# Token loads, low parts and the start of a conditioned transformer block: four edits of order

## The chip, the cores and the metric

The kernel runs on one core of one Trainium2 chip. Its time is the device time of one execution in microseconds (us); where several runs were made, their median is given. The engines are TensorE (PE; PEld is its weight load), VectorE (DVE), ScalarE (ACT), GpSimd (POOL) and SyncE (SP). SP here does nothing but issue DMA transfers; ACT and POOL issue some too. Each engine works through its own instructions in order.

## The reference

One block of a diffusion transformer on x of 2 x 2048 x 512 with a condition of 2 x 512, all in f32:

```
mod = silu(condition) @ Wada + bada            # 512 -> 6 * 512
sh_a, sc_a, gt_a, sh_m, sc_m, gt_m = split(mod, 6)
xm = layernorm(x, g1, be1) * (1 + sc_a) + sh_a
x  = x + gt_a * attention(xm)                  # 16 heads of 32, causal
xm = layernorm(x, g2, be2) * (1 + sc_m) + sh_m
x  = x + gt_m * (gelu(xm @ W1 + b1) @ W2 + b2) # 512 -> 2048 -> 512
```

attention(xm) is xm @ Wqkv (512 -> 1536) split into q, k and v, softmax(q k^T / sqrt(32)) v with the causal mask, and a projection with Wproj and bproj.

## The kernel before

**Stages.** The two batch rows run one after the other. For each: queries, keys and values are made (`Qkv.run`, L1138) while the first scores already run; then the attention phase; the projection of row 0 is done in row 1's start (L1531). At the end comes the MLP for both rows.

**Products.** A 512-wide product is split into halves and made by seven half products in place of eight (the four blocks of a matrix are A11, A12, A21, A22, and S1 to S4 are sums of them, L886). Weight sums are made on GpSimd, sums of tokens on VectorE. One unit of such a product is seven steps (`unit`, L1002) into three banks ps_a, ps_b and ps_c. Banks are emptied by ScalarE (first, direct) and VectorE (last).

**Qkv.run.** Four groups g of 512 tokens; in each, four units of keys and queries and two of values, 42 steps. After each step comes `tick` (L1145), which places other work by hand: at n = 3 the loads of the next group's tokens (`load_x`, L915, four tiles "x" from four buffers, on SP), at n = 10 to 13 their statistics on VectorE, at n = 15 and 25 their scaling on ScalarE (x, L964), at 18 and 28 the transposes on TensorE (ps_xt) with the modulation into xmT (L274), at 36 to 40 sums of tokens; also scores (`row.score`), and one load of stored keys or queries for the scores. `load_x` is called for g + 1 at n = 3 if it hasn't been yet. A group whose statistics, tiles or weights are late holds what stands behind it in its queue.

**hi and lo.** Keys and queries are stored as a rounded high part and a low part (`split`, L1061): hi is a cast on ScalarE (L1064), lo = value - hi is made at L1066, on VectorE for groups 0 and 1 and on GpSimd for groups 2 and 3. There are three hi buffers, so a fourth hi waits until the first is stored and its lo made. SP stores both to DRAM (L1031).

**Pieces.** MLP weights are summed ahead of time inside `Qkv.run` (class Pieces): `load` (L1222 to L1243) puts the loads of four blocks on SP, `add` puts sums on GpSimd (L1251) and stores to w1d or w2d (L1271). In `tick` (L1275) one or two of these operations are issued. A plan gives each piece the tick of its load and of its first sum. In row 1 the last piece (room_3) is loaded at tick 74 and summed from tick 80 on.

**Order.** Instructions passed through `mm`, `act` or `transpose` (L204 to L214) keep the order in which they are written on their engine; the others are placed by a scheduler. DMA transfers issued by SP and ACT share eight completion counters, one after the other in turn.

**The start** (L1360 to L1490). ScalarE issues loads of the condition and of g1, be1, g2, be2, b1, b2 into one tile `rows`, with `first`, a one-column Sqrt, at L136. SP loads the tokens of group 0, eight tiles of Wada (named vv, since they lie in room of vv), Wqkv's four blocks (wqk, L926) and the values' four (wv, L936). `rows` is transposed (ps_c, L1401) and copied to `cols`. ScalarE makes Silu of the condition from `cols` into sc (L1455); TensorE multiplies it with Wada (ps_mod, `modulation`, L1406), VectorE adds the bias (mr, L1425), TensorE turns the result into columns (ps_modt), and `scale_shift` (L1440) makes a and c, by which the transposed tokens become xmT (L269, L274). Then come the first products (ps_qk). GpSimd sums the weights column block by column block (L944).

The functions that the diff touches:

Of the kernel before, what the change touches and what calls it, by code (L numbers as in the profile page):

```python
# [8 lines left out]
F32 = mybir.dt.float32  # L9
# [8 lines left out]
P = 128  # L18
# [9 lines left out]
def dit_block_kernel(  # L28
# [104 lines left out]


    first = const.tile([P, 1], F32, tag="first", name="first")
    nc.scalar.activation(first, eps, AF.Sqrt)  # L136


    cols = const.tile([P, 64], F32, tag="cols", name="cols")
# [68 lines left out]
    def act(ins):  # L208

        return tc.keep_in_program_order(ins)  # L210
# [687 lines left out]
    class Qkv:  # L898
# [21 lines left out]
                xts.append(xt)  # L920
            self.xts[g] = xts

        def load_w(self, queue):
            for n, i, k in BASE:
                act(
                    queue.dma_start(  # L926
                        self.w[:, n], w_v[:, k * HK : (k + 1) * HK, i * D : (i + 1) * D]
                    )
                )

# [110 lines left out]
        def keys_and_queries(self, g, f, hp):  # L1041

            ops = self.operands(g)
            los = [self.lo_tile(hp) for _ in range(2)]

            def part(i, j):
                return los[i].bitcast(F32)[:, j * HALF_T : (j + 1) * HALF_T]

            def product(ps, n, new):
                for k in range(HK):  # L1050
                    mm(
                        ps, self.w[:, n, k, f * P : (f + 1) * P], ops[n][:, k],
                        start=new and k == 0, stop=k == HK - 1,
                        skip_group_check=not new,
                    )

            def first(ps, i, j):
                scale = HD**-0.5 if i == 0 else 1.0
                nc.scalar.activation(part(i, j), ps, AF.Copy, scale=scale)

            def split(i):  # L1061
                hi, lo = self.hi_tile(hp), los[i]
                d = lo.bitcast(F32)
                nc.scalar.copy(hi, d)  # L1064
                engine = nc.vector if g < 2 else nc.gpsimd
                engine.tensor_tensor(lo, d, hi.bitcast(F32), ALU.subtract)  # L1066
                self.stored(g, f, i, (hi, lo))

            def last(ps, i, j):
                d = part(i, j)  # L1070
                if i == 0:
                    nc.vector.scalar_tensor_tensor(
                        d, ps, HD**-0.5, d, ALU.mult, ALU.add
                    )
                    if j == 0:
                        split(0)
                else:
                    nc.vector.tensor_tensor(d, d, ps, ALU.add)

            def direct(ps, i, j):  # L1080
                first(ps, i, j)
                split(1)

            return self.unit(product, first, last, direct)
# [53 lines left out]
        def run(self, hp, also, early=()):  # L1138
# [3 lines left out]
            for g in range(NG):  # L1142
                at = [0]

                def tick():  # L1145
                    n, at[0] = at[0], at[0] + 1
                    if n >= self.STEPS:
                        return
                    if g + 1 < NG:
                        if n == 3 and g + 1 not in self.xts:  # L1150
                            self.load_x(g + 1)
                        if 10 <= n < 10 + MTT and g + 1 > row.b:
                            self.stats(g + 1, n - 10)
                        if n in (15, 25):
                            self.scaled(g + 1, n // 25)
                        if n in (18, 28):
                            self.norm(g + 1, n // 28)()
                        sums = {36: S1, 38: S2, 40: S3}
                        if n in sums:
                            self.token_sum(g + 1, sums[n])  # L1160
                    elif n == 28:

                        row.rows(0)
                        act(nc.scalar.activation(first, eps, AF.Exp))
                    if g > 0 and n == 2:
                        self.token_sum(g, A22)
                    if n > 9 and self.loads:
                        self.loads.pop(0)()
                    also(g, n)
                    if g > 0 and n >= 7:  # L1170


                        past, of = n - 6, self.STEPS - 7
                        if g == 1:
                            row.score(row.count(cum[0] * past / of, 0))
                        else:
                            past += of * (g - 2)
                            row.score(
                                row.count(
                                    cum[0] + (cum[2] - cum[0]) * past / (2 * of),  # L1180
                                    1 if g == 2 and n < 25 else 2,
                                )
                            )

                for u in range(C + 2):
                    if (g, u) in early:
                        for k, step in enumerate(self.plain(g, u, hp)):
                            step()
                            if k:
                                tick()  # L1190
                        self.token_sum(g, S3)
                        continue
                    if u < C:
                        steps = self.keys_and_queries(g, u, hp)
                    else:
                        steps = self.values(g, u - C)
                    for step in steps[:2] + late + steps[2:6]:
                        step()
                        tick()
                    late = steps[6:]  # L1200
# [159 lines left out]
    with pool("wada") as wp, pool("qkv0") as qp, pool("hl0") as hp, pool(  # L1360
        "ps_qkv0", bufs=6, space=PSUM
    ) as ps_mm:
        rows = wp.tile([n_rows, P], F32, tag="rows", name="rows")
        for r, n, src in (
            (0, n_cond, cond.rearrange("b (c p) -> (b c) p", p=P)),
            (r_g1, C, g1.rearrange("(c p) -> c p", p=P)),
# [3 lines left out]
            (r_b1, FC, b1.rearrange("(c p) -> c p", p=P)),  # L1370
            (r_b2, C, b2.rearrange("(c p) -> c p", p=P)),
        ):
            nc.scalar.dma_start(rows[r : r + n, :], src)
        wada_v = Wada.rearrange("(c p) f -> p c f", p=P)
        wada = {}

# [17 lines left out]
        qkv = Qkv(row, qp, ps_mm)  # L1394
        qkv.load_x(0)
        load_wada(0, 1)
        qkv.load_w(nc.sync)
        qkv.load_wv(hp, nc.sync)

        ps_c = ps_mm.tile([P, n_rows], F32, tag="mm", name="ps_c")  # L1400
        transpose(ps_c, rows)  # L1401
        nc.vector.tensor_copy(cols[:, :n_rows], ps_c)
        sc = wp.tile([P, C, HD], F32, tag="sc", name="sc")
        nc.vector.memset(sc, 0.0)

# [34 lines left out]
        def scale_shift(a, c, r_g, r_be, shift, scale):  # L1440
# [6 lines left out]
                )  # L1447
            nc.vector.tensor_tensor(c, c, mod[:, shift], ALU.add)

        for t in range(MTT):  # L1450
            qkv.stats(0, t)
        halves = [qkv.norm(0, 0, True)]

        act(
            nc.scalar.activation(  # L1455
                sc[:, :, :B], col(0, n_cond).rearrange("p (b c) -> p c b", c=C), AF.Silu
            )
        )
        picks()
        columns = modulation(0)  # L1460
        halves.append(qkv.norm(0, 1, True))
        columns()
        scale_shift(a1, c1, r_g1, r_be1, 0, 1)
        for k in range(0, C, 2):
# [862 lines left out]
```

## Time and profile before

| | |
|---|---|
| median of 3 runs | 2258.35 us (2256.87 to 2260.15) |
| profiled execution, own time | 2256.73 us |
| its span in the trace | 2255.0 us, 1.7 us lie outside the span |
| mean granted TensorE clock | 0.997 |
| TensorE busy | 2211.3 us, 98% |
| VectorE, ScalarE, GpSimd busy | 68%, 45%, 58% |

The page lists busy time and share of the span for each engine. In the chain of work that ended last, each instruction is followed back to what released it. In a timeline, rows have the start in us, the duration, the engine, the line, the operation with its tiles and sizes, the count of instructions grouped, and in brackets the idle time before with what ended it. A duration of a group runs from its first start to its last end. In the table by windows, each engine's column is its busy time with the number of instructions, then come the clock that TensorE was granted (1.00 is full), the share of DMA and the GB/s.

### The profile page before, as it was taken

The page shows a single profiled execution, that of the slowest core. Times are in us where ns is not written, and L with a number is a line of the kernel's source. Part 1 is how long each engine was busy: PE and PEld are TensorE (multiplying, and loading weights), DVE is VectorE, ACT ScalarE, POOL GpSimd, SP SyncE. Part 2 cuts the span into 40 slices and gives each one's busy share as a digit, 9 for nine tenths or more (in the row PEclk, how much of TensorE's full clock was granted, in tenths as well). Part 3 has the DMA queues.
Part 4 walks back from the last instruction along what each step waited for, and adds up shares of the span by engine and source line. Part 5 has one row for each costly group of instructions (what it writes and reads, how often), then busy time and mean ns, then how long its engine had stood idle before and what let it go on. Part 6 is the DMA issues. An engine that isn't in the chain of part 4 may idle for free.

```text
span 2255.0 us, 33464 instructions
## 1 busy us (share of the span) xinstructions
PE 2211.3 (98%) x12057; PEld 1432.2 (64%) x12057; DVE 1535.7 (68%) x3309; ACT 1004.6 (45%) x2012; POOL 1297.9 (58%) x807
## 2 busy tenths in 40 slices
PE   7999999999999999999999999999999999999998
PEld 6777555555543587855555555345787787688687
DVE  4668766777757666777577767663685586576576
ACT  4434555555564244365656555614322422332410
POOL 4253998998983695199989898444205204304210
PEclk9999999999999999999999999999999999999999
DMA  8877143231324799542324113363353354353433
GB/s 281 251 259 193 43 93 75 62 85 48 106 97 135 252 308 313 142 92 62 85 67 104 44 48 131 109 231 129 109 175 133 123 184 145 108 187 126 158 125 110
DMA packets 160510, 311.57 MB, mean 138 GB/s; under 512 B 16544, under 2 KB 48844, under 8 KB 158552
## 3 DMA queue, kind: packets, MB, share of 16 engines
q1 hardware_dynamic: 155488, 285.53, 41.8%
q0 software_dynamic: 4480, 23.36, 2.7%
q8 instruction: 95, 1.56, 0.3%
q14 instruction: 71, 0.58, 0.1%
q10 hardware_dynamic: 376, 0.55, 0.1%
HBM read 229.95 MB, written 87.29 MB: 141 GB/s over the span
## 4 chain that ended last, share of the span: by engine, by line
PE 89%; DVE 4%; DMA 2%; POOL 2%; ACT 1%; issue 1%; SPq 0%; DVEq 0%; ACTq 0%; POOLq 0%
PE ps_a L206 27%; PE st L206 18%; PE ps_b L206 12%; PE o L206 10%; PE s L206 9%; PE ps_c L206 4%; PE ps_o L206 4%; PE sm L206 3%; DVE junk L498 1%; POOL ee L695 1%; PE ps_xt L214 1%; DMA x<-in_x_dram 1%; ACT e L670 1%; DVE mx L504 1%; PE ps_o L214 1%
## 5 line engine op out<-in xcount | busy, mean ns | idle before, releaser
L670 ACT ACTIVATE e<-st 128x512 f32<-128x512 f32 (+1 forms) x1152 | 575.0, 579 | 362.4 <-PE st L206 321.3
L504 DVE TENSOR_REDUCE mx<-s 128x1 f32<-128x512 f32 x576 | 381.9, 686 | 199.0 <-PE s L206 197.9
L695 POOL TENSOR_TENSOR ee<-ee,e 128x2048 f32<-128x2048 f32 x106 | 485.8, 4583 | 10.3 <-ACT e L670 4.3
L206 PE MATMUL st<-qst,kst 128*128 128x512 f32 (+3 forms) x1280 | 408.7, 386 | 0.0
L206 PE MATMUL s<-kst,qst 128*128 128x512 f32 (+3 forms) x1046 | 382.2, 396 | 8.0 <-DVE mx L498 2.7
L206 PE MATMUL ps_a<-sum,w 128*128 128x256 f32 (+1 forms) x1088 | 328.8, 431 | 0.1
L206 PE MATMUL o<-e,vv 128*32 128x512 f32 (+3 forms) x2560 | 293.2, 537 | 0.3 <-POOL e L682 0.3
L206 PEld LDWEIGHTS st<-qst,kst 128*128 128x128 f32 x1280 | 228.5, 188 | 97.3 <-issue 65.7
L498 DVE CUSTOM_DVE_ANT_0 junk<-s,causal 128x128 bf16<-128x128 f32 (+3 forms) x470 | 220.7, 470 | 61.0 <-PE s L206 46.8
L1795 POOL TENSOR_TENSOR sum<-w 128x256 f32<-128x256 f32 x30 | 21.8, 727 | 397.1 <-DMA w<-w1d 203.1
L206 PEld LDWEIGHTS s<-kst,qst 128*128 128x128 f32 x1046 | 195.4, 189 | 72.4 <-DVE mx L504 15.4
L206 PEld LDWEIGHTS ps_a<-sum,w 128*128 128x128 f32 x1088 | 204.5, 190 | 40.1 <-issue 11.4
L695 POOL TENSOR_TENSOR ee<-e 128x2048 f32<-128x2048 f32 x42 | 192.5, 4583 | 43.5 <-ACT e L670 42.5
L206 PEld LDWEIGHTS <-sel 32*128 32x128 bf16 x1152 | 29.5, 91 | 197.0 <-issue 196.1
L2014 ACT ACTIVATE h<-h,cols 128x512 f32<-128x512 f32 x120 | 76.8, 710 | 136.3 <-DVE h L1716 136.3
L504 DVE TENSOR_REDUCE mx<-st 128x1 f32<-128x512 f32 x192 | 131.0, 682 | 0.5
L682 POOL TENSOR_SCALAR_AFFINE_SELECT e<-e 128x512 f32<-128x512 f32 x128 | 83.3, 669 | 67.2 <-ACT e L670 67.2
L206 PE MATMUL st<-fold,sel 32*128 32x512 bf16 (+1 forms) x1152 | 117.3, 372 | 1.2
L206 PEld LDWEIGHTS o<-e,vv 128*32 128x32 f32 x2560 | 59.1, 108 | 92.3 <-issue 72.8
L1716 DVE TENSOR_TENSOR h<-c,ps_b 128x256 f32<-128x256 f32 x90 | 37.9, 421 | 103.5 <-PE ps_b L206 103.0
L1066 POOL TENSOR_TENSOR lo<-lo,hi 128x512 fp32r<-128x512 f32 x32 | 40.7, 1274 | 114.2 <-ACT hi L1064 109.8
L206 PE MATMUL ps_b<-sum,w 128*128 128x256 f32 (+1 forms) x384 | 95.0, 383 | 0.0
(237 smaller groups left out, 3590.7 us busy)
## 6 DMA issues: line engine op xcount, KB each, us to landing
qst<-q SPq DMA_DIRECT2D x128, 256.0 KB
kst<-k SPq DMA_DIRECT2D x128, 256.0 KB
w<-w1d SPq DMA_DIRECT2D x32, 896.0 KB
w<-w2d SPq DMA_DIRECT2D x28, 1024.0 KB
w<-w2d SPq DMA_DIRECT2D x28, 768.0 KB
q<-hi SPq DMA_DIRECT2D x32, 256.0 KB
q<-lo SPq DMA_DIRECT2D x32, 256.0 KB
k<-hi SPq DMA_DIRECT2D x32, 256.0 KB
```

What stands on the lines that cost most here:

```text
L206: return tc.keep_in_program_order(nc.tensor.matmul(*args, **kw))
L214: return tc.keep_in_program_order(nc.tensor.transpose(dst, src, ident[:n, :n]))
L498: nc.vector.tensor_tensor_reduce(junk[:, :w], x, causal[:, QB - w :], 1.0, MASKED, ALU.add, ALU.max, m,)
L504: self.vector(nc.vector.tensor_reduce(m, x, axis=AX.X, op=ALU.max))
L670: act(nc.scalar.activation(e4[:, h, :w], sts[h][:, :w], AF.Exp))
L682: nc.gpsimd.affine_select(d, d, pattern=[[0, HC], [1, P]], compare_op=ALU.is_ge, fill=0.0, base=0, channel_multiplier=-1,)
L695: act(nc.gpsimd.tensor_tensor(dst, x, y, ALU.add))
L1066: engine.tensor_tensor(lo, d, hi.bitcast(F32), ALU.subtract)
L1716: act(nc.vector.tensor_tensor(dst, x, y, ALU.add))
L1795: act(engine.tensor_tensor(dst, u, v, op))
L2014: nc.scalar.activation(d[j], d[j], AF.Gelu, bias=col(r_b1 + half * HF + fs[j], 1))
```

## The change

Four edits of order, none of what is computed:

- **Tokens.** At n = 30 of group g, `tick` also loads the tokens of group g + 2, behind the last transposes (n = 28) of the tiles whose buffers they take. At n = 3 of the next group the load is then left out. The tokens of group 1 are loaded as before.
- **Low parts.** For groups 2 and 3 the subtraction on GpSimd is passed through `act` and so keeps its written place among GpSimd's other pinned work.
- **Start: condition.** A tile `rows_c` of its own takes the condition first (the load into `rows` stays), and ScalarE's loads are pinned, with a Silu of one column behind that of be1. `rows_c` is transposed into ps_1; Silu of it, straight from PSUM, and a Sqrt of one column behind it stand ahead of the statistics. The transpose of `rows` moves behind the second half of the first tokens. 36 transposes of the identity (`busy`) into ps_w go to TensorE before and behind ps_1.
- **Start: weights.** Wqkv's blocks are loaded by columns, 0 to 127, 128 to 255 and 256 to 511, in twelve transfers where there were four.

```diff
@@ -133,7 +133,6 @@
 
 
     first = const.tile([P, 1], F32, tag="first", name="first")
-    nc.scalar.activation(first, eps, AF.Sqrt)
 
 
     cols = const.tile([P, 64], F32, tag="cols", name="cols")
@@ -920,11 +919,12 @@
                 xts.append(xt)
             self.xts[g] = xts
 
-        def load_w(self, queue):
+        def load_w(self, queue, f=slice(0, D)):
             for n, i, k in BASE:
                 act(
                     queue.dma_start(
-                        self.w[:, n], w_v[:, k * HK : (k + 1) * HK, i * D : (i + 1) * D]
+                        self.w[:, n, :, f],
+                        w_v[:, k * HK : (k + 1) * HK, i * D + f.start : i * D + f.stop],
                     )
                 )
 
@@ -1063,7 +1063,9 @@
                 d = lo.bitcast(F32)
                 nc.scalar.copy(hi, d)
                 engine = nc.vector if g < 2 else nc.gpsimd
-                engine.tensor_tensor(lo, d, hi.bitcast(F32), ALU.subtract)
+                ins = engine.tensor_tensor(lo, d, hi.bitcast(F32), ALU.subtract)
+                if g >= 2:
+                    act(ins)
                 self.stored(g, f, i, (hi, lo))
 
             def last(ps, i, j):
@@ -1146,6 +1148,8 @@
                     n, at[0] = at[0], at[0] + 1
                     if n >= self.STEPS:
                         return
+                    if n == 30 and g + 2 < NG:
+                        self.load_x(g + 2)
                     if g + 1 < NG:
                         if n == 3 and g + 1 not in self.xts:
                             self.load_x(g + 1)
@@ -1361,6 +1365,7 @@
         "ps_qkv0", bufs=6, space=PSUM
     ) as ps_mm:
         rows = wp.tile([n_rows, P], F32, tag="rows", name="rows")
+        rows_c = wp.tile([n_cond, P], F32, tag="rowsc", name="rowsc")
         for r, n, src in (
             (0, n_cond, cond.rearrange("b (c p) -> (b c) p", p=P)),
             (r_g1, C, g1.rearrange("(c p) -> c p", p=P)),
@@ -1370,7 +1375,11 @@
             (r_b1, FC, b1.rearrange("(c p) -> c p", p=P)),
             (r_b2, C, b2.rearrange("(c p) -> c p", p=P)),
         ):
-            nc.scalar.dma_start(rows[r : r + n, :], src)
+            if not r:
+                act(nc.scalar.dma_start(rows_c, src))
+            act(nc.scalar.dma_start(rows[r : r + n, :], src))
+            if r == r_be1:
+                act(nc.scalar.activation(first, eps, AF.Silu))
         wada_v = Wada.rearrange("(c p) f -> p c f", p=P)
         wada = {}
 
@@ -1394,12 +1403,19 @@
         qkv = Qkv(row, qp, ps_mm)
         qkv.load_x(0)
         load_wada(0, 1)
-        qkv.load_w(nc.sync)
+        for f0, f1 in ((0, 1), (1, 2), (2, C)):
+            qkv.load_w(nc.sync, slice(f0 * P, f1 * P))
         qkv.load_wv(hp, nc.sync)
 
-        ps_c = ps_mm.tile([P, n_rows], F32, tag="mm", name="ps_c")
-        transpose(ps_c, rows)
-        nc.vector.tensor_copy(cols[:, :n_rows], ps_c)
+        ps_w = ps_sp.tile([P, P], F32, tag="s", name="ps_w")
+
+        def busy(n):
+            for _ in range(n):
+                transpose(ps_w, ident)
+
+        busy(6)
+        ps_1 = ps_sp.tile([P, n_cond], F32, tag="s", name="ps_1")
+        transpose(ps_1, rows_c)
         sc = wp.tile([P, C, HD], F32, tag="sc", name="sc")
         nc.vector.memset(sc, 0.0)
 
@@ -1447,18 +1463,23 @@
                 )
             nc.vector.tensor_tensor(c, c, mod[:, shift], ALU.add)
 
+        act(
+            nc.scalar.activation(
+                sc[:, :, :B], ps_1.rearrange("p (b c) -> p c b", c=C), AF.Silu
+            )
+        )
+        act(nc.scalar.activation(first, eps, AF.Sqrt))
+        busy(30)
         for t in range(MTT):
             qkv.stats(0, t)
         halves = [qkv.norm(0, 0, True)]
 
-        act(
-            nc.scalar.activation(
-                sc[:, :, :B], col(0, n_cond).rearrange("p (b c) -> p c b", c=C), AF.Silu
-            )
-        )
         picks()
         columns = modulation(0)
         halves.append(qkv.norm(0, 1, True))
+        ps_c = ps_mm.tile([P, n_rows], F32, tag="mm", name="ps_c")
+        transpose(ps_c, rows)
+        nc.vector.tensor_copy(cols[:, :n_rows], ps_c)
         columns()
         scale_shift(a1, c1, r_g1, r_be1, 0, 1)
         for k in range(0, C, 2):
```

## The prediction

> **What bounds the kernel now.** I read the busy shares first, then the chain of work that ended last, then TensorE's waits.
>
> ```profile
> PE 2211.3 (98%) x12057; PEld 1432.2 (64%) x12057; DVE 1535.7 (68%) x3309; ACT 1004.6 (45%) x2012; POOL 1297.9 (58%) x807
> PE 89%; DVE 4%; DMA 2%; POOL 2%; ACT 1%; issue 1%; SPq 0%; DVEq 0%; ACTq 0%; POOLq 0%
> ```
>
> TensorE is busy 98% of the span and carries 89% of the chain. No other engine is near it, and the change removes no product. So it can only move the little idle time that TensorE has, and the stretches at half clock behind such idle time. Both are in three places: the start, 118 us (row 0) and 873 us (row 1).
>
> ```profile
> PE ps_c L214 <- DMA rows<-in_L_cond_b_dram: 7.4, 1, 7.4
> PE ps_xt L214 <- ACT x L964: 5.6, 4, 3.8
> ```
>
> These are rows of the waits of 0 to 40 us and of 700 to 1000 us: total, times, longest. The first is not the start's real bound, since ps_c only feeds columns; the timeline is. Here are TensorE, ScalarE and SyncE's DMA issues at the start (start, us, engine and line, instructions, idle time before):
>
> ```profile
> 9.19 0.48 PE L214 MATMUL ps_xt<-ident,x 128*128 128x128 f32 x1 [1.50 <-ACT x L964]
> 11.58 2.75 PE L206 MATMUL ps_mod<-vv,sc 128*32 128x512 f32 x16
> 14.26 1.09 PE L214 MATMUL ps_xt<-ident,x 128*128 128x128 f32 x8
> 18.12 7.13 PE L206 MATMUL ps_qk<-xmT,wqk 128*128 128x512 f32 x16 [1.78 <-DVE xmT L269]
> 27.86 1.10 PE L206 MATMUL ps_a<-t,wqk 128*128 128x256 f32 x4 [0.89 <-POOL wqk L944]
> ...
> 2.40 0.32 ACTq L1373 DMA_DIRECT2D rows<-in_L_cond_be_dram  x1
> 4.32 1.28 ACT L136 ACT_TABLE_LOAD   x1 [4.32 <-DMA x<-in_x_dram]
> 5.61 0.20 ACT L136 ACTIVATE first<-eps 128x1 f32<-128x1 f32 x1
> 7.42 0.30 ACT L224 ACTIVATE rstd<-mv,eps 128x4 f32<-128x4 f32 x1 [1.61 <-DVE mv L221]
> 8.32 1.52 ACT L964 ACTIVATE x<-x,shift,rstd 128x512 f32<-128x512 f32 x2 [0.60 <-DVE shift L226]
> 11.15 0.21 ACT L1455 ACTIVATE sc<-cols 128x8 f32<-128x8 f32 x1
> ...
> 4.22 3.79 SPq L1391 DMA_DIRECT2D vv<-in_L_cond_Wada_dram  x8
> 12.18 0.37 SPq L936 DMA_DIRECT2D wv<-in_L_cond_Wqkv_dram  x1
> ```
>
> The reader is to see a chain on ScalarE: table load, rstd, scaled tokens, then the first transpose at 9.19, and 8.93 us later the first product of keys and queries (18.12).
>
> **The change, part by part. The start.** The hardware DMAs share eight completion counters in turn, and an issue waits until the load before it on its counter has landed. The trace shows it: ScalarE's table load at 4.32 stands behind a row load of b1 that waited for a token load, and the third value-weight load (12.18) was issued when the seventh Wada load had landed. The changed kernel pins the row loads and the first two activations to written order. As built, ScalarE's queue holds: condition twice, g1, be1, a Silu of one column, then g2, be2, b1, b2, then the Silu of the condition, Sqrt, rstd and the scaled tokens. The extra load turns the counters by one place, so that g2, be2, b1 and b2 now stand on those of the first, third, fifth and seventh Wada loads, and all of ScalarE's work stands behind the wait of b2. The seventh Wada load landed at 12.18. Before it DMA had a gap, in half-microsecond windows (busy time of each engine left to right, clock, DMA share, GB/s):
>
> ```profile
> 5.00:5.50 0.50, 0.00 (x0) 0.00 (x0) 0.27 (x2) 0.50 (x1) 0.41 (x1) 1.00 0.69 162
> 5.50:6.00 0.50, 0.00 (x0) 0.00 (x0) 0.32 (x1) 0.30 (x2) 0.00 (x0) 1.00 0.74 99
> 6.00:6.50 0.50, 0.00 (x0) 0.00 (x0) 0.47 (x2) 0.00 (x0) 0.00 (x0) 1.00 0.56 175
> 7.00:7.50 0.50, 0.11 (x1) 0.14 (x1) 0.47 (x4) 0.08 (x1) 0.00 (x0) 1.00 1.05 393
> ```
>
> Against 390 GB/s the three lack 228, 291 and 215 GB/s for 0.5 us each, 367 KB or 0.94 us. Without the counters' early waits SyncE issues sooner and the gap closes: landing at 12.18 - 0.94 = 11.2 (bounds 10.8, if the first issue at 4.22 moves up by its 1.35 us of waits, and 12.2, if nothing moves). Then: issue of b2 0.32, Silu 0.21, table load 1.28, first 0.20, rstd at 13.25; from rstd to the first transpose 9.19 - 7.42 = 1.77, so 15.0; then 8.93 to the first product, with one transpose (ps_c, 1.09 / 8 = 0.14) moved into it: 24.1, against 18.12, **+6.0**. The stall of 0.89 at 27.86, on GpSimd's weight sums, goes: the weights now come by columns and the products start 6 us later. That leaves **+5.1**. Bounds: +7.0 (landing at 12.2 and the stall kept); +2.5 (landing at 10.8, and the clock full from the first transpose on: eight transposes in 1.09 instead of the 2.4 from 9.19 to 11.58, ps_mod in 1.92 instead of 2.75).
>
> The 37 transposes of an identity run on TensorE while it would idle, done by 13 us at the latest (eight fill 9.19 to 11.58, 0.30 us each, so 37 take at most 11 us from about 2). They cost nothing, and I give them no gain: 2 us of idle time or more follow before 15.0, and at 118 us 2.75 us of idle time were enough for half clock (below). ScalarE's table load there stays one of 1.28.
>
> The Trainium skill's page "ScalarE: Activation LUTs", section "What ACT_TABLE_LOAD costs", puts a switch of table at 1.28 us of load and about 1.38 of drain; in this trace the row of 4.32 has the load, and the next activation starts 0.01 us behind it. By the page the start would be 1.4 us later than my sum.
>
> The page "TensorE: Matmul & The Clock Gate", section "Part 4: PE-mode transpose", says that transposes don't count as busy for the clock. By it ps_mod would run wholly at half clock. The trace speaks against it: at half clock its 16 matmuls would take twice the 1.92 us of 113.90 (below), 3.84, and they took 2.75, so the clock rose in the midst of them.
>
> **Row 0, near 118 us.** SyncE, VectorE, TensorE and the clock:
>
> ```profile
> 107.57 4.91 SPq L1230 DMA_DIRECT2D kst<-in_L_cond_W_dram  x4
> 112.58 1.84 SPq L919 DMA_DIRECT2D x<-in_x_dram  x4
> ...
> 118.51 0.69 DVE L218 BATCH_NORM_STATS2 stat<-x 128x6 f32<-128x512 f32 x1 [0.90 <-DMA x<-in_x_dram]
> ...
> 113.90 1.92 PE L206 MATMUL ps_mod<-vv,sc 128*32 128x512 f32 x16
> 119.86 0.80 PE L206 MATMUL s<-kst,qst 128*128 128x512 f32 x1 [2.75 <-DVE mx L498]
> ...
> 119.00:120.00 1.00, 0.14 (x1) 0.14 (x1) 1.00 (x5) 0.00 (x0) 0.00 (x0) 0.56 1.06 322
> 120.00:125.00 5.00, 5.00 (x12) 4.01 (x13) 3.58 (x10) 0.82 (x2) 1.45 (x2) 0.50 0.56 198
> 125.00:126.00 1.00, 1.00 (x4) 0.76 (x4) 0.72 (x3) 0.00 (x0) 0.92 (x2) 0.53 0.36 131
> ```
>
> The tokens of group 3 are issued behind four weight pieces; VectorE's statistics wait for them, and the maxima behind them hold TensorE 2.75 us. By the clock's column (third from the right) half clock lasts from 119.1 to 125.9, 6.8 us; from TensorE's start on that is (125.9 - 119.86) / 2 = 3.0 us lost. In the changed kernel the token load (tick 30) stands ahead of the four pieces, 5.0 us sooner. The third token tile, late at 118.51, is there at 113.5, before VectorE needs it. Its statistics also move earlier among the maxima, but wait for nothing. 2.75 + 3.0 = **-5.7** (-4.5 to -6.5: part of the stall kept, or the maxima before it sooner too). The pieces come 1.9 us later; GpSimd sums them behind other work.
>
> **Row 1, near 873 us.** SyncE, TensorE, GpSimd, ScalarE, clock:
>
> ```profile
> 861.25 0.93 SPq L1239 DMA_DIRECT2D vv<-in_L_cond_W_dram  x2
> 865.36 1.84 SPq L919 DMA_DIRECT2D x<-in_x_dram  x4
> ...
> 876.68 0.33 PE L214 MATMUL ps_xt<-ident,x 128*128 128x128 f32 x1 [3.79 <-ACT x L964]
> 884.26 1.89 PE L206 MATMUL ps_a<-t,wqk 128*128 128x256 f32 x8
> ...
> 867.51 1.27 POOL L1066 TENSOR_TENSOR lo<-lo,hi 128x512 fp32r<-128x512 f32 x1 [2.06 <-ACT hi L1064]
> 869.33 1.28 POOL L1251 TENSOR_TENSOR vv<-vv,kst 128x512 f32<-128x512 f32 x1 [0.55 <-DMA kst<-in_L_cond_W_dram]
> 881.55 0.56 POOL L1271 DMA_DIRECT2D w2d<-vv  x1
> 882.82 1.28 POOL L1251 TENSOR_TENSOR qst<-qst 128x128 f32<-128x128 f32 x3
> 887.73 3.73 POOL L1066 TENSOR_TENSOR lo<-lo,hi 128x512 fp32r<-128x512 f32 x3
> ...
> 881.39 0.62 ACT L1064 CAST hi<-lo 128x512 fp32r<-128x512 f32 x1 [0.44 <-POOL kst L1251]
> ...
> 877.00:880.00 3.00, 2.62 (x11) 2.43 (x11) 0.40 (x1) 2.71 (x6) 2.92 (x3) 0.50 0.94 188
> ```
>
> The same move brings the tokens 4.1 us forward (865.36 to 861.25), ahead of eight W2 pieces. The statistics no longer wait, but still stand in VectorE's order, one eviction of the product sooner; I take half of the wait of 3.79 as gone (1.9; bounds nothing and all of it), with the first transpose at 874.8. The half clock of 877 to 880 and about 0.4 us around it goes (3.4 / 2 = 1.7, estimated to go since 1.9 us of idle time are under the 2.75 at 118 us): TensorE would be **3.6 us** ahead near 881.
>
> The other edit takes it back. Each low part (lo) waits for its high part (hi, ScalarE); there are three tiles for hi, so a new hi waits until GpSimd has made an earlier lo. Before, the scheduler had put three lo ahead of the last W2 piece's sums (867.51 is the third). With the lo pinned to written order, the program has eleven sums ahead of the first lo, and four more ahead of the second. GpSimd now waits for W2 data which come 1.9 us later: sums from about 871.2 instead of 869.33, eleven in 881.55 - 869.33 = 12.2 us, so the first lo at 883.4 to 884.7, then one sum of kst and three of qst (in before from the end of the store at 882.1 to 884.1, 2.0 us) and the second lo (1.27): 888.0 at the latest, 886.7 at the earliest; I take 887.8. ScalarE's fourth and fifth hi wait for those, and in its queue stand ahead of two evictions (lo, 0.38 each) that TensorE needs for its ps_a: hi 0.62, evictions 0.7, so TensorE goes on at 889.1. In before it was at the same product at 885.1 (half of the row at 884.26): **+4.0**. It then has idled 7.5 us, and half clock follows, for 3.4 us (row 1 before) to 6.0 (row 0): half of it, +1.7 to +3.0; I take **+2.2**, nearer row 1's. Together **+6.2** for row 1. Bounds: -3.6 if nothing is held, +8.5 if the next hi, behind seven stores, holds TensorE again.
>
> **Sum.** +5.1 - 5.7 + 6.2 = +5.6 us on the profiled execution's 2256.73 (span 2255.0), so 2262.3; the median of the runs shown is 2258.35, 1.62 above it: **2264.0**. A measurement of this kernel tells about 0.2%, 4.5 us, from no change.
>
> **The rivals.**
>
> A second stall, chance 0.13. Behind the second lo stand one sum of 0.47 and seven stores (3.8 us) before the third (893.4), and hi 6 waits for it: TensorE loses 2 to 5 us more, or the start's later bound holds: 2268.
>
> The low parts hold nothing (the other side: not slower), 0.14. The evictions that TensorE needs pass before the waiting hi, so that GpSimd's new order costs only GpSimd. For it: GpSimd is busy 58%, and in before a hi at 881.39 already waited for GpSimd with TensorE unharmed. Against it: the queues run in order, and the lag of 12 us is longer than any slack here. It decides from the point where the first two lo end before 883. Row 1 is then -3.6: 2258.35 + 5.1 - 5.7 - 3.6 = 2254.2.
>
> ScalarE isn't held at the start, 0.07: the row loads pass without waiting for Wada. The first product then comes about 2 us sooner instead: 2258.35 - 2 - 5.7 + 6.2 = 2256.9. For it: Wada may land sooner than its issues tell. With the rival before, 2247: 0.04.
>
> The clock rises late at the start: no transpose counts for it, and ps_mod's 16 matmuls take 2 x 1.92 = 3.84 instead of 2.75, +1.1: 2265.1, chance 0.05. This is the rule of the Trainium skill's page on TensorE named above.
>
> The token load lands no sooner, since its buffers are still read at tick 30 and SyncE waits there: 0.03, 2264.0 + 5.7 = 2269.7.
>
> **How the numbers follow.** My forecast (2259 to 2268) has 0.54, of it 0.33 above 2262.9, with the late clock's 0.05, the second stall's 0.13 and the unmoved load's 0.03: slower 0.54. Faster, below 2253.8: 0.04 and half of the 0.14, 0.11. The rest, 0.35, is within 0.2%. The range, 2254 to 2270, leaves out the 0.04, some 0.07 of the rival around 2254.2, and the ends of the second stall.
>
> **What would show it.** Right: ScalarE's Silu of the condition at about 11.5 us, the first transpose of tokens near 15, the first ps_qk near 24; no wait of TensorE for VectorE's mx near 118, and clock 1.00 there; near 880 TensorE waiting 6 to 8 us for a lo on ScalarE, itself behind hi and GpSimd's W2 sums, and clock 0.50 after it. Wrong: a first ps_qk before 18; GpSimd's lo running between the sums; TensorE without a wait between 875 and 890; a new wait on the W2 pieces or on weights at 25 to 30 us.

## The result and the profile after

The changed kernel takes 2272.09 us (median of 5 runs, 2271.35 to 2273.83); the kernel before took 2258.85 in runs beside it (5 runs). The ratio is 1.0066 with a 95% interval of 1.0055 to 1.0077: some 15 us slower. The forecast was 2264.0, with a range up to 2270. The profiled execution took 2272.53 us, with a span of 2270.8 us; the mean granted clock fell from 0.997 to 0.993.

The page of the changed kernel, busy times and the chain that ended last:

```profile
PE 2220.8 (98%) x12094; PEld 1438.6 (63%) x12094; DVE 1530.7 (67%) x3309; ACT 1002.4 (44%) x2012; POOL 1295.5 (57%) x807
PE 85%; DVE 4%; POOL 3%; DMA 2%; ACT 1%; issue 1%; SPq 0%; DVEq 0%; ACTq 0%; POOLq 0%
```

TensorE is busy 9.5 us longer, but 7.1 us of that are the 37 short transposes (1.76 to 8.91 us), made while it would idle, so the busy time alone doesn't tell where the loss is. Where the 15.8 us of span went is read from TensorE's order, which is the same in both kernels behind the start: for each matmul, its start after less its start before is TensorE's lateness.

| TensorE's instruction | before | after | lateness |
|---|---|---|---|
| first transpose of tokens | 9.19 | 15.54 | 6.4 |
| first ps_qk | 18.12 | 25.78 | 7.7 |
| first ps_a behind it | 25.09 | 35.54 | 10.5 |
| ps_mod in row 0 | 113.90 | 125.25 | 11.4 |
| ps_modt in row 0 | 126.19 | 131.59 | 5.4 |
| a ps_a in row 1 | 825.69 | 831.59 | 5.9 |
| a score (s) before the tokens | 869.26 | 876.67 | 7.4 |
| a ps_a behind the transposes | 880.92 | 882.27 | 1.4 |
| ps_b behind the stall | 886.22 | 897.04 | 10.8 |
| s behind the next stall | 899.29 | 913.91 | 14.6 |

So the change has five effects: the start +10.5, row 0 -6.0, the tokens of row 1 -4.5 (5.9 to 1.4, with 1.5 us of new waits for maxima, among which the statistics now stand), the stall behind them +9.4 and the next one +3.8 (0.7 us of it is still half clock behind the first). That is 13.2; of the other 2.6, 1.2 lie behind the last matmuls, and the rest crept in between in waits of under 1 us.

The start after, TensorE and then ScalarE (timeline as in the prediction):

```profile
1.76 1.54 PE L213 MATMUL ps_w<-ident 128*128 128x128 f32 x6 [1.76 <-POOL ident masks.py:199]
3.43 5.48 PE L213 MATMUL ps_w<-ident 128*128 128x128 f32 x30
15.54 0.48 PE L213 MATMUL ps_xt<-ident,x 128*128 128x128 f32 x1 [6.62 <-ACT x L964]
17.93 3.52 PE L205 MATMUL ps_mod<-vv,sc 128*32 128x512 f32 x16
25.78 9.93 PE L205 MATMUL ps_qk<-xmT,wqk 128*128 128x512 f32 x16 [2.13 <-DVE xmT L268]
```

```profile
3.73 0.20 ACT L1382 ACTIVATE first<-eps 128x1 f32<-128x1 f32 x1
6.96 0.26 ACTq L1380 DMA_DIRECT2D rows<-in_L_cond_g_dram  x1
8.71 0.26 ACTq L1380 DMA_DIRECT2D rows<-in_L_cond_be_dram  x1
10.60 1.63 ACTq L1380 DMA_DIRECT2D rows<-in_L_cond_b_dram  x2
12.34 0.18 ACT L1467 ACTIVATE sc<-ps 128x8 f32<-128x8 f32 x1 [8.41 <-DMA rows<-in_L_cond_be_dram]
12.54 1.28 ACT L1471 ACT_TABLE_LOAD   x1
13.83 0.20 ACT L1471 ACTIVATE first<-eps 128x1 f32<-128x1 f32 x1
13.94 0.28 ACT L223 ACTIVATE rstd<-mv,eps 128x4 f32<-128x4 f32 x1
```

The reader is to see the four issues of row loads spread over 5 us, each waiting, and the Silu only behind the last, as forecast. Then TensorE's clock, third column from the right:

```profile
7.00:11.00 4.00, 1.91 (x15) 1.67 (x13) 0.78 (x7) 0.00 (x0) 0.00 (x0) 0.99 1.00 362
11.00:17.00 6.00, 1.24 (x5) 0.94 (x6) 0.34 (x2) 4.19 (x8) 0.00 (x0) 0.50 0.70 193
17.00:21.00 4.00, 4.00 (x21) 1.19 (x19) 0.00 (x0) 0.60 (x1) 2.82 (x4) 0.50 1.00 325
21.50:24.50 3.00, 2.14 (x17) 1.83 (x17) 1.67 (x5) 0.00 (x0) 2.20 (x4) 1.00 1.08 379
25.00:31.00 6.00, 5.22 (x6) 2.19 (x7) 6.00 (x11) 1.93 (x4) 5.98 (x9) 0.50 0.51 184
```

This column reads 1.00 up to the first change that a trace has on record, here at 7.55 us; the rise to full clock is seen in the identity transposes themselves, which start 0.213 us apart up to then and 0.109 us apart behind it. Full clock is gone at 11, comes back at 21.2, and is lost once more for the first 5.7 us of ps_qk, which take 9.93 us instead of 7.13.

Row 0, where TensorE waited and ran at half clock before (ps_modt is at 131.59 here):

```profile
128.00:137.00 9.00, 9.00 (x46) 7.64 (x45) 8.21 (x21) 5.44 (x11) 4.32 (x7) 1.00 0.74 207
```

TensorE is busy throughout, and the clock is full.

Row 1, near 890 us, TensorE, ScalarE and GpSimd:

```profile
880.06 1.04 PE L213 MATMUL ps_xt<-ident,x 128*128 128x128 f32 x8
885.62 1.03 PE L205 MATMUL ps_a<-t,wqk 128*128 128x256 f32 x4
894.74 2.08 PE L205 MATMUL ps_a<-t,wqk 128*128 128x256 f32 x4 [8.10 <-ACT lo L1059]
...
912.04 0.73 PE L205 MATMUL s<-kst,qst 128*128 128x512 f32 x1 [2.61 <-DMA qst<-q]
```

```profile
890.37 0.62 ACT L1064 CAST hi<-lo 128x512 fp32r<-128x512 f32 x1 [7.00 <-POOL lo L1066]
893.51 0.62 ACT L1064 CAST hi<-lo 128x512 fp32r<-128x512 f32 x1 [2.52 <-POOL lo L1066]
894.03 0.65 ACT L1059 ACTIVATE lo<-ps_a 128x256 f32<-128x256 f32 x2
```

```profile
876.82 1.27 POOL L1255 TENSOR_TENSOR vv<-vv,kst 128x512 f32<-128x512 f32 x1 [20.56 <-DMA q<-hi]
...
889.08 1.26 POOL L1066 TENSOR_TENSOR lo<-lo,hi 128x512 fp32r<-128x512 f32 x1
890.29 0.73 POOL L1255 TENSOR_TENSOR kst<-kst 128x256 f32<-128x256 f32 x1
890.98 1.28 POOL L1255 TENSOR_TENSOR qst<-qst 128x128 f32<-128x128 f32 x3
892.21 1.27 POOL L1066 TENSOR_TENSOR lo<-lo,hi 128x512 fp32r<-128x512 f32 x1
```

This is the chain of the forecast: eleven sums, a low part, four sums, a low part, each freeing a hi; behind the second hi the evictions that TensorE waits for. TensorE no longer waits for scaled tokens here (880.06 has no idle time). What the sum had left to a rival is the second wait, 2.61 us for queries that come back from DRAM.

### The profile page after: what moved, and what is told of

It is laid out like the page before. It is cut to its first block, busy times and chain, and to the rows that moved or that the text cites. A ratio compares the mean times of both kernels' runs of the same rounds, so it can differ in the third digit from the quotient of the medians.

```text
span 2270.8 us, 33548 instructions
## 1 busy us (share of the span) xinstructions
PE 2220.8 (98%) x12094; PEld 1438.6 (63%) x12094; DVE 1530.7 (67%) x3309; ACT 1002.4 (44%) x2012; POOL 1295.5 (57%) x807
## 4 chain that ended last, share of the span: by engine, by line
PE 85%; DVE 4%; POOL 3%; DMA 2%; ACT 1%; issue 1%; SPq 0%; DVEq 0%; ACTq 0%; POOLq 0%
PE ps_a L205 25%; PE st L205 18%; PE ps_b L205 11%; PE o L205 10%; PE s L205 9%; PE ps_c L205 3%; PE sm L205 3%; PE ps_o L205 2%; POOL ee L694 1%; DVE junk L497 1%; PE ps_xt L213 1%; ACT e L669 1%; DVE mx L503 1%; PE ps_o L213 1%; DVE stat L217 0%
## 5 line engine op out<-in xcount | busy, mean ns | idle before, releaser
L694 POOL TENSOR_TENSOR ee<-ee,e 128x2048 f32<-128x2048 f32 x106 | 486.1, 4586 | 10.1 <-ACT e L669 4.2
L205 PEld LDWEIGHTS ps_a<-sum,w 128*128 128x128 f32 x1088 | 204.5, 190 | 40.1 <-issue 11.4
```

The lines of the kernel that those rows point to most:

```text
L205: return tc.keep_in_program_order(nc.tensor.matmul(*args, **kw))
L694: act(nc.gpsimd.tensor_tensor(dst, x, y, ALU.add))
```

## The experiments

**The three parts alone, and two together.** The theory: the losses and gains lie in separate places. The rivals tie them together.

The token load alone (a_alone), on the kernel before:

```diff
+                    if n == 30 and g + 2 < NG:
+                        self.load_x(g + 2)
```

> The kernel before with the token load at n = 30 alone. Theory (three separate places): TensorE's wait at 119 us and the half clock behind it go (-5.5 us in the trace after), and so does the wait for scaled tokens at 873 us (-4.3): about 2249 us. GpSimd keeps three low parts ahead of the last W2 piece's sums, so ScalarE is not held. Rival (the token load itself brings the stall near 885, since the W2 pieces come 1.9 us later): -5.5 - 4.3 and then a wait of 5 us or more on a low part: 2255 or more.

Measured: 2252.75 us, ratio 0.9982 (0.9971 to 0.9993). That is 3.9 us under the kernel before beside it (2256.66), where the theory had 9.8: the sign is the theory's, the size the rival's, though TensorE isn't held near 885. In the trace TensorE gains 5.6 us across 118 us and 5.9 across 873, but each time it loses 1.6 us just ahead in waits for VectorE's maxima, among which the statistics now stand; 2.5 us more are lost in small steps from 200 to 850 us. Its start, with the same instructions as before, was 2.8 us later, with half clock in ps_qk.

The pinned low parts alone (b_alone):

```diff
-                engine.tensor_tensor(lo, d, hi.bitcast(F32), ALU.subtract)
+                ins = engine.tensor_tensor(lo, d, hi.bitcast(F32), ALU.subtract)
+                if g >= 2:
+                    act(ins)
```

> The kernel before with the low parts of groups 2 and 3 pinned on GpSimd alone. Theory: the first low part stands behind eleven W2 sums, the second behind four more; with W2 data from 869.3 us the second ends near 886, TensorE waits some 2 us near 885 and again about 2.6 for the next queries, with up to 2 us of half clock: +5 (2 to 8), 2264 us. Rival (the order is harmless as long as the W2 data aren't late): within 1 us of 2258.9.

Measured: 2265.01 us, 1.0042 (1.0028 to 1.0056), 8.4 us over the kernel before beside it: slower at the upper end, and not harmless without late W2 data. The wait stands elsewhere than expected. ScalarE and GpSimd of this kernel:

```profile
880.86 0.62 ACT L1064 CAST hi<-lo 128x512 fp32r<-128x512 f32 x1 [9.94 <-POOL lo L1066]
881.38 0.29 ACT L224 ACTIVATE rstd<-mv,eps 128x4 f32<-128x4 f32 x1
...
879.56 1.26 POOL L1066 TENSOR_TENSOR lo<-lo,hi 128x512 fp32r<-128x512 f32 x1
```

The hi that waits for the first low part stands ahead of rstd here, so that the scaling of tokens waits too: TensorE's wait for scaled tokens is 11.7 us where it was 3.8. The second wait that was expected, for queries, is 0.3 us here.

The start alone (c_alone): the diff without the two edits above.

> The kernel before with the edits of the start alone. Theory: TensorE is 11 us late by 96 us, as in the trace after, and nothing gives it back: 2269.5 us (2268.5 to 2271). Rival (the wait at 119 us for tokens shrinks, since the loads are less late than the products): up to 2.75 us and its half clock come back, 2264.

Measured: 2264.43 us, 1.0034 (1.0021 to 1.0046): the rival. TensorE is 12.3 us late at 97 us, and 7.8 behind 125 us: since it comes later to the place where it waited 2.75 us for tokens, it waits 0.50 there, and stays at full clock. The lateness of the start and the token load draw on the same 5 us.

Token load and start, without the pinning (ac):

```diff
-                ins = engine.tensor_tensor(lo, d, hi.bitcast(F32), ALU.subtract)
-                if g >= 2:
-                    act(ins)
+                engine.tensor_tensor(lo, d, hi.bitcast(F32), ALU.subtract)
```

> The changed kernel without the pinning of low parts. Theory: the stall of 8.1 us near 886, its half clock and the wait of 2.6 for queries go, 13.4 us together: 2258.7 us. Rival (the stall comes from the moved token load, which delays the W2 pieces): 2266 or more.

Measured: 2258.78 us, 1.0006 (0.9998 to 1.0015), 13.3 under the changed kernel. In the two traces the two waits of row 1, with the half clock behind them, differ, and nothing else by over 1 us: by the pinning TensorE ends 13.4 us later here.

**The low parts.** One more hi tile in row 1 (h_hi4), all else as changed:

```diff
-            return hp.tile([P, MT], F32R, tag="hi", name="hi", bufs=3)
+            return hp.tile([P, MT], F32R, tag="hi", name="hi", bufs=3 + self.row.b)
```

> The changed kernel with a fourth tile for high parts in row 1. Theory (ScalarE waits for a hi tile that GpSimd's late low part still reads): the hi that waited for the second low part now waits for the first, which ends 3.1 us sooner: TensorE's wait of 8.1 us falls to about 5, 2269 us. Rival (ScalarE or TensorE waits for something else than the tile): no change, 2272.

Measured: 2266.1 us, 1.0043 (1.0031 to 1.0056). TensorE's waits of 870 to 930 us in this kernel:

```profile
PE ps_a L205 <- ACT lo L1059: 4.0, 1, 4.0
PE s L205 <- DMA qst<-q: 2.9, 1, 2.9
```

The wait for the eviction is halved, 8.1 to 4.0, but not in the way that the theory had it. ScalarE and GpSimd of this kernel:

```profile
882.50 0.62 ACT L1064 CAST hi<-lo 128x512 fp32r<-128x512 f32 x1 [3.42 <-POOL lo L1066]
885.63 0.62 ACT L1064 CAST hi<-lo 128x512 fp32r<-128x512 f32 x1 [1.54 <-POOL lo L1066]
886.16 0.38 ACT L1059 ACTIVATE lo<-ps_a 128x256 f32<-128x256 f32 x1
...
868.90 1.28 POOL L1255 TENSOR_TENSOR vv<-vv,kst 128x512 f32<-128x512 f32 x1 [15.86 <-DMA kst<-in_L_cond_W_dram]
```

The tile is used: one more hi passes, and the next (882.50) waits for the first low part only. But the eviction that lets TensorE go on (886.16, TensorE at 886.59) still stands behind a hi that waits for the second low part. What changed is when that low part is made: SyncE issued the W2 loads at 858.73, not 869.02, and GpSimd's sums start 7.9 us sooner than in the changed kernel, while TensorE came to this place 4.1 us sooner. The difference, 3.8 us, is nearly the whole gain of 4.1. So the rows show that a hi waits for the tile that a low part still reads; what the tile by itself is worth, this run does not show.

(In this profiled execution the start was 3 to 4 us faster than in that of the changed kernel with the same instructions there, at full clock in ps_qk; so the time fell by more than the wait.) The wait for queries stays. In the changed kernel SyncE stores the third low part at 898.92, as soon as it is made, and issues the loads of queries behind it, up to 906.87; that these loads end the wait is read from the rows, and no run takes this wait away by itself.

**The start.** The theory: ScalarE's queue behind the four row loads is the whole lateness. Four row loads on GpSimd's queue (s1_rows_gp), without the pinning; lines cut to what differs:

```diff
-            act(nc.scalar.dma_start(rows[r : r + n, :], src))
+            if r <= r_be1:
+                act(nc.scalar.dma_start(rows[r : r + n, :], src))
+            else:
+                act(nc.gpsimd.dma_start(rows[r : r + n, :], src))
```

> The changed kernel without the pinning of low parts, and with the row loads of g2, be2, b1 and b2 on GpSimd's queue in place of ScalarE's. Theory (ScalarE's queue, held by row loads that wait for Wada loads, is the whole lateness of the start): Silu of the condition near 5 us, first transposes of tokens near 9, the first ps_qk at 17 to 18 in place of 25, so 7 to 10 us under the 2258.8 of the kernel without the pinning: 2249 to 2252 us. Rival (Wada's landing, the columns of Wqkv or the identity transposes set the start): first ps_qk at 22 or later, 2256 or more.

Measured: 2257.16 us, 0.9998 (0.9989 to 1.0007). The first half of the theory holds: the Silu is at 3.83, the first transpose at 9.42, the first ps_qk at 17.71. The time doesn't follow; TensorE, 8.2 us ahead of ac at 22 us, is 2.6 ahead at 38. TensorE and VectorE of this kernel:

```profile
17.71 8.78 PE L205 MATMUL ps_qk<-xmT,wqk 128*128 128x512 f32 x16 [2.27 <-DVE xmT L268]
30.90 1.67 PE L205 MATMUL ps_a<-t,wqk 128*128 128x256 f32 x4 [2.69 <-POOL wv L949]
...
19.42 3.32 DVE L997 TENSOR_TENSOR t<-xmT,t 128x512 f32<-128x512 f32 x2
22.66 3.07 DVE L1495 COPY pick<-pickc 128x512 f32<-128x512 f32 x1
```

ps_qk is again partly at half clock. And VectorE's copy pick, 0.95 us in before, takes 3.07, so that the next statistics, rstd and the evictions behind it on ScalarE are late; the wait of 2.69 is put down to GpSimd by the profile, but ScalarE's rstd at 30.24, which had waited 3.1 us for VectorE, ends it.

The same with pick moved to tick 24 (s1p):

```diff
-        act(nc.vector.tensor_copy(pick, pickc.unsqueeze(3).to_broadcast([P, 2, B, P])))
...
+            if (g, n) == (0, 24):
+                act(
+                    nc.vector.tensor_copy(
+                        pick, pickc.unsqueeze(3).to_broadcast([P, 2, B, P])
+                    )
+                )
```

> The kernel without pinning and with four row loads on GpSimd's queue, with VectorE's copy pick (3.07 us there) moved to tick 24. Theory (that copy, beside GpSimd's sums, makes the statistics of group 1 late, and rstd holds ScalarE's evictions): rstd of group 1 near 27 us instead of 30.2, TensorE's wait of 2.7 us at 30.9 and half clock behind it go: 2257.2 - 2.7 - 2 = 2252.5 us (2251 to 2254). Rival (the token loads of group 1 behind twelve weight loads are late): 2257 again.

Measured: 2250.8 us, 0.9973 (0.9964 to 0.9983), 1.7 us under the theory's time. The profiled execution, at 2253.94 us the slowest of ten, doesn't show the theory's path: two token sums took 6.06 us there, and rstd was at 30.86 again. The trace of s1pf below, which has pick moved too, does: its rstd is at 27.16. So pick is one of several instructions that meet the same obstacle.

No identity transposes (s2_no_busy), without the pinning: the lines `busy(6)` and `busy(30)` are left out.

> The changed kernel without the pinning of low parts and without the 36 identity transposes. Theory: they warm TensorE at 5 to 7 us, and it is cold again at 11 to 14, before the first tokens at 15, so nothing changes: 2258.8 us within 1.5. Rival (they set when the half clock falls, and with it the half clock in ps_qk): 2.5 us or more off, up or down.

Measured: 2263.71 us, 1.0032 (1.0021 to 1.0044), 4.9 over ac: the theory is refuted. But the clock isn't the cause. VectorE and GpSimd of this kernel:

```profile
27.03 4.49 DVE L997 TENSOR_TENSOR t<-xmT 128x512 f32<-128x512 f32 x1
32.05 3.29 DVE L997 TENSOR_TENSOR t<-xmT,t 128x512 f32<-128x512 f32 x1
35.93 0.67 DVE L997 TENSOR_TENSOR t<-xmT,t 128x512 f32<-128x512 f32 x1
...
27.26 3.70 POOL L949 TENSOR_TENSOR wv<-wv 128x512 f32<-128x512 f32 x3
30.92 0.54 POOL L1392 DMA_DIRECT2D mr<-in_L_cond_bada_dram  x1
```

The first token sum, which takes 0.68 us in ac, ends here 0.6 us behind the point where GpSimd stops summing to issue a DMA (30.92). ps_modt was 0.2 us later than in ac, and the sums fell into a stretch without a pause. To test that, GpSimd is made to wait for the token sums (s2g):

```diff
+        guard = wp.tile([P, 1], F32, tag="guard", name="guard")
+        act(nc.gpsimd.tensor_copy(guard, qkv.t[A22][:, 0, :1]))
         qkv.value_weight_sums()
```

> The kernel without pinning and without identity transposes, with GpSimd's value-weight sums behind a one-column copy that waits for VectorE's third token sum. Theory (the 4.9 us that the kernel without the transposes lost come from VectorE's token sums, which took 4.5 and 3.3 us instead of 0.7 beside GpSimd's sums): each token sum of the first group takes under 1 us, TensorE's wait of 2.5 us near 40 goes, 2259 to 2260.5 us. Rival (the clock without the transposes is the loss): 2263.7 us again.

Measured: 2256.3 us, 0.9997 (0.9988 to 1.0006), below the forecast, and as fast as ac with no identity transposes at all:

```profile
26.93 0.68 DVE L997 TENSOR_TENSOR t<-xmT 128x512 f32<-128x512 f32 x1
28.14 0.67 DVE L997 TENSOR_TENSOR t<-xmT,t 128x512 f32<-128x512 f32 x1
29.40 0.67 DVE L997 TENSOR_TENSOR t<-xmT,t 128x512 f32<-128x512 f32 x1
```

Weights in four whole loads (s3_whole_w), without the pinning: `qkv.load_w(nc.sync)` in place of the loop over columns.

> The changed kernel without the pinning of low parts, Wqkv's blocks whole in 4 loads instead of 12 by columns. Theory: ScalarE sets the start, the weights are there before it either way: first ps_qk at 25, 2258.8 us within 1.5. Rival (the twelve loads hold SyncE's queue, and the value weights and next tokens behind it): 2 us or more faster.

Measured: 2260.52 us, 1.0015 (1.0006 to 1.0024) against ac's 1.0006 (0.9998 to 1.0015): the intervals overlap, so the runs don't tell whether the columns bring nothing or some 2 us. TensorE waits 1.47 and 1.90 us near 37 us, where ac waits 0.36. The profile puts the first down to GpSimd's sums; but as in s1_rows_gp it ends with the eviction behind ScalarE's rstd, which at 35.08 had waited 1.90 us for VectorE.

**The clock.** 14 identity transposes between ps_modt and the first ps_qk, on ac (ac_fill) and on the token load alone (a_fill):

```diff
         scale_shift(a1, c1, r_g1, r_be1, 0, 1)
+        ps_v = ps_mm.tile([P, P], F32, tag="mm", name="ps_v")
+        for _ in range(14):
+            transpose(ps_v, ident)
```

> The kernel without pinning, with 14 identity transposes between ps_modt and the first ps_qk, where TensorE idles 1.8 us. Theory (the idle stretch throws TensorE to half clock in ps_qk, and transposes count as work for the clock): ps_qk in 7.0 us instead of 10.1, 2258.8 - 3 = 2256 us. Rival (transposes don't count): half clock in ps_qk again, 2258.8 or more.

> The kernel before with the token load at n = 30, and the same 14 identity transposes between ps_modt and the first ps_qk. Theory: half clock in ps_qk, which its profile had for 3.4 us and the profile of before hadn't, never comes: up to 1.7 us under the 2252.75 of the token load alone, 2251.5 us. Rival (the transposes delay ps_qk): up to 1 us over it.

Measured: 2256.22 us, 1.0000 (0.9991 to 1.0009), and 2250.78 us, 0.9973 (0.9964 to 0.9983). On ac, before the edit and with it:

```profile
25.00 10.12 PE L205 MATMUL ps_qk<-xmT,wqk 128*128 128x512 f32 x16 [1.78 <-DVE xmT L268]
```

```profile
22.79 1.73 PE L213 MATMUL ps_v<-ident 128*128 128x128 f32 x14
25.09 7.13 PE L205 MATMUL ps_qk<-xmT,wqk 128*128 128x512 f32 x16 [0.58 <-DVE xmT L268]
```

ps_qk starts at the same time and takes 3.0 us less; behind the next wait (1.20 us, at 35.15) TensorE is still 1.4 us ahead. One pair of traces wouldn't show that the transposes did it, since the clock's steps move from run to run. But in all three traces with the 14 transposes (s1pf is the third) ps_qk takes 7.13 us, and without them in only three of thirteen (before, b_alone, h_hi4). So they very likely keep the clock. By the times neither kernel can be told from the one without them: the intervals overlap.

**The pieces together.** The repaired start with the 14 transposes (s1pf), and the repaired start with the low parts pinned again (b_s1p):

> The kernel without pinning, four row loads on GpSimd's queue, pick moved, and 14 identity transposes between ps_modt and the first ps_qk. Theory: the half clock of 17.2 to 24.0 us in the profile of the kernel without the 14 transposes goes (its cost there 2 us): 2249 us. Rival (the repaired start is held by something else): 2250.8 again.

> The changed kernel, low parts pinned, with the repaired start (four row loads on GpSimd's queue, pick moved). Theory: the loss at the low parts stands by itself, about 13.4 us over the kernel with the same start and without the pinning (2250.8): 2264 us; waits near 880 of 8 us for lo and 2.6 for the next queries. Rival (with an earlier TensorE it waits shorter or longer by the lateness of the start, 7 us): 2257 or 2271.

Measured: s1pf 2250.2 us, 0.9971 (0.9960 to 0.9982), in its profiled execution 2248.92 with no half clock until the last microseconds; b_s1p 2266.87 us, 1.0045 (1.0032 to 1.0059), with waits of 7.3 us for the eviction and 1.9 for queries. b_s1p is 16.1 us above s1p, where 13.4 was forecast; the two were not run side by side, and their intervals allow 11 to 21. So the pinned low parts cost about as much behind an early start as behind a late one. s1pf and s1p can't be told apart by the time, nor from a_fill.

## Why the prediction was wrong

- **Direction and places: right.** Slower was the likeliest case, and the start, row 0, the tokens of row 1 and the low parts are where the traces differ.
- **The step that failed: the start, +5.1.** It measured +10.5 at the first ps_a and +10.1 behind the stall that went. The mechanism, ScalarE behind row loads that wait for Wada, was right (s1_rows_gp takes it away: first ps_qk at 17.71). The first transpose came 0.5 us later than worked out (15.54 against 15.0). The miss is in what follows: "then 8.93 to the first product", and that product as before. Measured: 10.24 us to the first ps_qk, in the main since ps_mod took 3.52 us instead of 2.75, and then ps_qk 9.93 instead of 7.13, for half clock. I had carried over the clock that before had. How much of this a run pays is in part chance: with the same instructions at the start, the first ps_a is later than in before by 10.5 us in the changed kernel, 9.9 in ac and 11.2 in c_alone, but by 6.5 in h_hi4, whose ps_qk are at full clock. In ac_fill they are, too.
- **The identity transposes cost nothing and gain nothing: wrong by the runs without them (+4.9), but not by the clock.** They shift ps_modt against GpSimd's sums; s2g has no such transposes and is as fast as ac.
- **The stall at the weight sums, -0.89: it goes, but I had misread it.** The profile puts the wait at 27.86 of before down to GpSimd. It ends with ScalarE's eviction, which stood behind a table load:

```profile
25.91 1.28 ACT L224 ACT_TABLE_LOAD   x1
27.40 0.36 ACT L1059 ACTIVATE lo<-ps_a 128x256 f32<-128x256 f32 x1
```

  In all sixteen traces TensorE's weight load for this product starts 0.07 us behind the end of that eviction; GpSimd's last update before it lies 0.02 to 4.4 us back. The changed kernel has made this switch of table at 12.54 already, so the columns of Wqkv needn't be the reason that the wait went. A new wait of 0.58 us (38.87), for the next eviction, gives most of the gain back.
- **Row 0, -5.7: right** in the trace (11.4 to 5.4). But c_alone got 4.5 us of it without the token load, from lateness alone, and in a_alone the token load without the lateness brought 5.6 less a new wait of 1.6: a sum of separate terms counted it once, and would have been wrong for the start by itself.
- **Row 1, +6.2: right in kind and nearly in size.** The stall was forecast at 7.5 us and measured at 8.10; tokens and stall together make 5.9 to 10.8 in the table, +4.9. Left out was the wait for queries behind late low parts, 2.61 us with half clock after it, 10.8 to 14.6 in the table, +3.8 with the first stall's last 0.7. It was there as the rival of a second stall, through another cause (the next hi).
- **The sum.** Measured +10.5 - 6.0 + 4.9 + 3.8 and 2.6 of small waits, 15.8; forecast +5.1 - 5.7 + 6.2. The start is off by 5.4, and the second stall by 3.8.
- The range ended at 2270, since the start's later bound (+7.0, itself without half clock in ps_qk) and the second stall were not taken together.

## What to carry to other kernels

Before a DMA issue is put into a fixed place on a compute engine's queue, look at which earlier transfer its completion counter belongs to: everything behind it waits for that transfer. Pinning an instruction to its written order takes from the scheduler the place that kept the queue moving; ask what stands ahead of it as written, and which buffer waits for it. And a duration taken from before holds only at the clock it had: where a step is moved behind idle time, give the products after it a half-clock price, and bound the time from above with all such prices at once.

## What the runs showed of the hardware

- The clock rises and falls in steps whose place moves from run to run: in before the first ps_qk took 7.13 us, in ac 10.12, and behind the same row loads in h_hi4 7.13. The Trainium skill's page "TensorE: Matmul & The Clock Gate", section "What's actually happening", says that the gate looks at a free-running window of 3.41 us; the half-clock stretches of before (119.1 to 125.9 and 3.4 us at 877) are two windows and one.
- Transposes count as work for the clock. In the changed kernel TensorE had nothing but identity transposes and one of the condition up to 8.91 us, and at 7.55 us the distance of their starts fell from 0.213 to 0.109 us. The 14 in ac_fill, a_fill and s1pf go with full clock in ps_qk each time. Section "Part 4: PE-mode transpose" of the Trainium skill's page "TensorE: Matmul & The Clock Gate" says that they don't count in the same way; the measurements decide.
- A switch of activation table cost 1.28 us, and the next activation followed 0.01 us later (rows 12.54 and 13.83 of the changed kernel); the 1.38 us of drain that the Trainium skill's page "ScalarE: Activation LUTs", section "What ACT_TABLE_LOAD costs", adds didn't show.
- A VectorE sum of two SBUF tiles beside GpSimd's sums took 4.49 us instead of 0.67. The Trainium skill's page "SBUF — State Buffer", section "Who interferes with whom", has the two share a port, taken by one for a whole instruction; here GpSimd kept it over three instructions back to back (3.70 us), until it paused to issue a DMA.
